# One kernel, two edits: decay attention's norm and sending steps in other slots, and the squares of the local and sink norms summed in four column groups of TensorE

## The chip, the cores and the metric

One core of one Trainium2 chip runs the whole program. The metric is device time of one execution in microseconds (us). The engines are named as in the profile: PE is TensorE's matrix multiplication and PEld its weight loads, DVE is VectorE, ACT is ScalarE, POOL is GpSimd, SP is SyncE, which here only issues DMAs.

## The reference

A chain of sixteen residual blocks on an array of 4096 tokens of 128 channels, `x = x + block(_layernorm(x))`. Three kinds of block matter here.

```
def _layernorm(x, axis=-1, eps=1e-05):
    m = jnp.mean(x, axis=axis, keepdims=True)
    v = jnp.var(x, axis=axis, keepdims=True)
    return (x - m) / jnp.sqrt(v + eps)

# local attention (L0_ffn): run twice, two layers each time
    x = x + local_attention(...) @ wo
    h = shift_token(x)
    h = (h - mu) / jnp.sqrt(var + 1e-05) * lg + lb      # norm of the half step
    ...

# decay attention (L1_attn_b), followed by a mixture of experts (L1_ffn)
    scores = jnp.einsum('bqhd,bkhd->bhqk', q, k) * scale
    decay = jnp.exp(-alpha * lag * DT)
    attn = jax.nn.softmax(scores * decay, axis=-1)

# sink attention (L2_attn_b)
    x = rmsnorm(h, attn_norm_scale)
    h = h + attention(x, ..., sinks)
    x = rmsnorm(h, moe_norm_scale)
```

## The kernel before

Tokens stand along the free axis: a tile is 128 channels (partitions) by 512 tokens, and there are eight such chunks, `NCH = 8`. The stages run one after the other as in the reference. Inside a stage the order of the work is written out by hand: a loop over slots, in each of which a few steps of different chunks are recorded, and every engine executes its own instructions in the recorded order. So a step's place in that order decides what is queued behind it on each engine.

A norm is three steps. `centre_step` (line 1759) multiplies a chunk by `cent` (identity minus 1/128) on PE, copies the result out of PSUM on ACT and squares it, on POOL or, with `square=True`, on ACT. `spread_step` (line 1774) multiplies the squares by `mean`, a 128 x 128 matrix of 1/128, on PE. So every one of the 128 output rows is the same row of 512 variances; ACT takes Ln and then Exp of minus one half of it, on 128 x 512 each, into the tile `nrs`. The third step, `scale`, multiplies the chunk by `nrs` on DVE.

Local attention is `local_attend` (line 3358). One slot `m` is half a batch: scores, weights, an output, projections for later slots, and at its end `chunk_steps(m)`. There a chunk's norm steps stand in three successive slots: slots 9, 10, 11 plus 4c for the norm of x (`norm_x_step`, chunks 5 to 7 and only in the first layer of a pair, since the stage before has done chunks 0 to 4), and slots 6 to 9 plus 4c for the norm of the half step (`norm_of_half`, chunks 0 to 6; chunk 7's runs in `local_ffn`). The stage is run four times.

Sink attention is `window_attention` (line 3160). A slot `n` is one unit of 128 queries by 128 keys, 128 units in all, 16 to a chunk. `before(c, i)` are the three steps of the norm ahead of it, whose `spread_step` with `twice=True` makes two results (two Ln, two Exp); `after(c, i)` are those of the norm behind it.

Decay attention is `decay` (line 2952), with its slots in `small_stage` (line 2797). There are 64 units, 8 to a chunk, one scored per slot. Units of even slots (kind 0) are multiplied by the decay out of PSUM on DVE, four instructions of 128 x 512, and one slot later exponentiated on ACT in one of 128 x 2048; units of odd slots (kind 1) are exponentiated out of PSUM on ACT, four of 128 x 512. A chunk's steps stand in slots relative to its first unit: `guard` (two reductions on DVE) at 1, `project` at -6, and so on, and the norm of x at -9, -8, -7. When a chunk is finished, `out` adds it to x, and `lead`, here `Sending.steps` (line 3637), follows in eleven steps: norm (three), `compare`, `choose`, `place`, `turn`, and four of `scatter`, which send the chunk's tokens to the experts' rows by indirect DMAs on POOL. `compare` and `choose` rank the experts in a string of some twenty small DVE instructions. `later` (line 2816) places these steps at the slot of the chunk's last weighing plus 4, 5, ..., 14.

PSUM has eight banks, shared out per stage; in decay six serve scores and everything else, so PE can be little more than a slot ahead of the engines that empty them.

SP carries the weight loads of the stages (line 615), each waiting until the buffer of an earlier stage is free, and in the first local layer 66 copies that fill two rooms in HBM for the experts' rows (`fill_rooms`, line 2114).

Of the kernel before, what the change touches and what calls it, by code (L numbers as in the profile page):

```python
# [17 lines left out]
P = 128  # L18
B, T, C = 16, 256, 128
NT = B * T  # L20
CH = 512
NCH = NT // CH
# [1627 lines left out]
class Fast(Net):  # L1650
# [120 lines left out]
            self.gt(sq, dst, dst, ALU.mult)  # L1771
        return sq

    def spread_step(self, pool, sq, bank, eps="eps5", twice=False):


        pv = self.bank(bank)
        self.mm(pv, self.k["mean"], sq)
        out = []
        for n in range(2 if twice else 1):  # L1780
            rs = pool.tile([P, CH], F32, tag=f"nrs{n}", name="nrs", bufs=2)
            if n:
# [8 lines left out]
    def norm_steps(self, pool, src, dst, bank, g=None, b=None, eps="eps5", copy=None, square=False):  # L1791


        held = {}

        def centre():
            held[0] = self.centre_step(pool, src, dst, bank, copy, square)

        def spread():
            held[1] = self.spread_step(pool, held[0], bank, eps)  # L1800
# [10 lines left out]
    def norm_x_step(self, pool, c, i, bank="ps", copy=None):  # L1811

        if c in self.led:
            return
        if i == 0:
            s = self.chunk(c)
            self.norms[c] = self.norm_steps(pool, self.x[:, s], self.ha[:, s], bank, copy=copy)
        self.norms[c][i]()

    def slots(self, n, *steps, last=(), every=1):  # L1820
# [976 lines left out]
    def small_stage(self, w, units, steps, tiles, evict, finish=None, group=1):  # L2797

# [7 lines left out]
        nc = self.nc  # L2806
        many = 2 * len(units)
        with ExitStack() as st:
# [5 lines left out]
            steps = [(first + i * group, lambda c, i=i: self.norm_x_step(p, c, i, "s")) for i in range(3)] + list(steps)  # L2814

            def later(n, i, f, c):

# [87 lines left out]
            def out(args):  # L2905
                slot, c = args
                pz = self.bank("s")
                self.mm(pz, w["Wo"], ots.pop(c))
                x = self.x[:, self.chunk(c)]
                if "bo" in w:  # L2910
                    self.stt(x, pz, w["bo"], x, ALU.add, ALU.add)
                else:
                    self.tt(x, x, pz, ALU.add)
                for i, f in enumerate(lead):
                    later(slot, (2 if finish else 4) + i, f, c)

            order = [None, join, turn, out]
            with self.share(s=6, o=2), self.tc.manual_schedule():
# [33 lines left out]
    def decay(self, w):  # L2952
# [4 lines left out]
        with ExitStack() as st:  # L2957
# [58 lines left out]
                (-2, lambda c: queries_by_edge(c, 0)), (0, lambda c: queries(c, 1)), (2, lambda c: queries_by_edge(c, 1)),  # L3016
            ]
            units = [(0, 0, 0), (0, 1, 1), (1, 1, 0), (1, 0, 1)]
            self.small_stage(w, units, steps, tiles, evict)

    def guard(self, stage, c, q, k):
        self.peak(stage, 0, c, q)
# [137 lines left out]
    def window_attention(self, w, h, n1, ns2):  # L3160
# [3 lines left out]
        with ExitStack() as st:  # L3164
# [134 lines left out]
            def before(c, i):  # L3299

                s = self.chunk(c)
                if i == 0:
                    held["sq"] = self.centre_step(p1, self.x[:, s], h[:, s], "s", square=True)
                elif i == 1:
                    held["rs"] = self.spread_step(p1, held["sq"], "s", twice=True)
                else:
                    r1, r2 = held["rs"]
                    self.stt(n1[:, s], h[:, s], w["ns1"], r2, ALU.mult, ALU.mult)
                    self.tt(h[:, s], h[:, s], r1, ALU.mult)

            def after(c, i):

                s = self.chunk(c)
                if i == 0:
                    held["sq"] = p1.tile([P, CH], F32, tag="nsq", name="nsq", bufs=2)
                    self.act(held["sq"], h[:, s], AF.Square)
                elif i == 1:
                    held["rs"] = self.spread_step(p1, held["sq"], "s")
                else:
                    self.stt(n1[:, s], h[:, s], ns2, held["rs"], ALU.mult, ALU.mult)  # L3320

            with self.share(s=4, o=4), self.tc.manual_schedule():
                self.logs()
                for n in range(-14, len(units) + 16):
                    if 0 <= n < len(units):
                        score(n)
                        later(n + 1, masked, n)
                    for f, args in (*due.pop(n, []), *due.pop(("last", n), [])):
                        f(*args)
                    if n % 2:  # L3330
                        for i in (n - 3, n - 2):
                            if 0 <= i < len(units):
                                weigh(i, n)
                        continue
# [12 lines left out]

    def local_begin(self):
        pass
# [8 lines left out]
    def local_attend(self, w, z, hs, last):  # L3358
# [6 lines left out]
        with ExitStack() as st:  # L3365
# [156 lines left out]
            def chunk_steps(m):  # L3522

                def due(slot):
                    c, rest = divmod(m - slot, 4)
                    return c if rest == 0 and 0 <= c < NCH else None

                if not last:
                    for i in range(3):
                        if (c := due(i - 9)) is not None:  # L3530
                            self.norm_x_step(p, c, i, "w")
                for slot in (-6, 5):
                    if (c := due(slot)) is not None:
                        self.shift(hs[:, self.chunk(c)], z[:, self.chunk(c)])

                for i in range(4):
                    if (c := due(6 + i)) is not None and c < NCH - 1:
                        if i == 0:
                            steps[1] = self.norm_of_half(p, "w", w, hs[:, self.chunk(c)])
                        steps[1][i]()  # L3540

            with self.share(w=3, s=4, o=1), self.tc.manual_schedule():
# [21 lines left out]
                    if within(m + 5, NTILE):  # L3564
                        project(m + 5)

    def norm_of_half(self, pool, bank, w, s):

        held = {}

# [1 line left out]
            held[0] = self.centre_step(pool, s, s, bank)  # L3572

        def spread():
            held[1] = self.spread_step(pool, held[0], bank)

        return [
            centre, spread, lambda: self.stt(s, s, w["lg"], held[1], ALU.mult, ALU.mult),
# [265 lines left out]
```

## Time and profile before

| what | value |
|---|---|
| median of 3 runs | 4233.71 us (4231.14 to 4234.19) |
| the profiled execution | 4216.97 us |
| its span, first to last instruction | 4215.2 us |
| PE busy | 3849.9 us, 91% |
| DVE, ACT, POOL busy | 61%, 55%, 44% |
| TensorE clock granted, mean | 0.951 |

| stage, loop alone | from about, to about (us) |
|---|---|
| local attention, four times | 140 to 440, 520 to 790, 1140 to 1440, 1470 to 1750 |
| decay attention | 2173 to 2450 |
| sink attention | 2900 to 3345 |

How to read it: a group is all instructions of one line, engine and pair of operands; most instructions are recorded at the line of a small helper (L504 is `mm`, L528 `act`, L531 `tt`, L534 `gt` on POOL, L543 `stt`), so a group is known by its tiles. A float32 matmul shows as two PE records. In a timeline a line is one run of like instructions: start, duration of the run, engine, line, operands, how many records, and in brackets the idle time ahead of it with what ended it. In a table of stretches the columns are the stretch, its length, the busy time of PE, PEld, DVE, ACT and POOL with their numbers of instructions, the granted TensorE clock, the DMA engines' share and GB/s.

### The profile page before, as it was taken

To read this page: it belongs to the slowest core of one execution; us is meant where nothing else is said; L and a number is where in the kernel's file an instruction comes from. 1 tells how busy PE (TensorE), PEld (TensorE's weight loads), DVE (VectorE), ACT (ScalarE), POOL (GpSimd) and SP (SyncE) were. 2 spreads that over 40 slices of the span, in tenths; PEclk is the share of its full clock that TensorE was granted. 3 is DMA by queue.
4 is the path that set the end of the run, shared out by engine and by line. 5 is a ranking of instruction groups with operands and counts; after the bars stand their busy time and mean duration, and the time that the engine had idled before them with its cause. 6 is when DMAs were issued, how large, how long until landed. Compare 5 with 4: busy or idle time off the path is not lost. (4 is left out here: it accounts for less than half of the span.)

```text
span 4215.2 us, 73089 instructions
## 1 busy us (share of the span) xinstructions
PE 3849.9 (91%) x28742; PEld 2195.1 (52%) x28742; DVE 2557.5 (61%) x4503; ACT 2314.2 (55%) x4485; POOL 1854.9 (44%) x1632
## 2 busy tenths in 40 slices
PE   7999999988899999985989879888999999899878
PEld 3555466465465456554965469543444344455333
DVE  4775576364577377464346633556877677486474
ACT  6666466555766466553456634444555554774532
POOL 4764365232566176326433434454555454321251
PEclk8999999988999999997999979999999999999989
DMA  1800000000000000004920058100000000000000
GB/s 61 345 2 1 11 2 1 20 1 1 20 1 1 3 1 1 1 6 142 320 76 12 16 180 297 41 19 16 1 1 1 3 1 10 6 2 19 6 0 21
DMA packets 78400, 176.38 MB, mean 42 GB/s; under 512 B 12606, under 2 KB 39108, under 8 KB 77920
## 3 DMA queue, kind: packets, MB, share of 16 engines
q1 hardware_dynamic: 65568, 148.40, 10.2%
q0 software_dynamic: 9120, 18.51, 1.3%
q8 instruction: 229, 3.75, 0.4%
q10 hardware_dynamic: 3360, 4.72, 0.4%
q14 instruction: 123, 1.01, 0.1%
HBM read 118.28 MB, written 54.20 MB: 41 GB/s over the span
## 5 line engine op out<-in xcount | busy, mean ns | idle before, releaser
L528 ACT ACTIVATE pt<-ps 128x512 f32<-128x512 f32 x640 | 339.9, 600 | 327.6 <-PE ps L504 326.4
L504 PE MATMUL ps<-hb,w 128*128 128x512 f32 (+1 forms) x960 | 461.0, 613 | 3.7 <-issue 3.3
L504 PE MATMUL ps<-w,hb 128*128 128x512 f32 (+2 forms) x896 | 403.8, 572 | 23.5 <-DVE t L531 18.6
L534 POOL TENSOR_TENSOR t<-t,t 128x512 f32<-128x512 f32 x256 | 319.8, 1271 | 161.1 <-DVE t L531 140.6
L531 DVE TENSOR_TENSOR t<-ps,tab 128x512 f32<-128x512 f32 x512 | 317.7, 682 | 84.6 <-ACT sq L528 81.1
L534 POOL TENSOR_TENSOR t<-t,ss 128x1024 f32<-128x1024 f32 x128 | 243.7, 1904 | 192.8 <-ACT ss L528 191.6
L504 PEld LDWEIGHTS ps<-hb,w 128*128 128x128 f32 (+1 forms) x960 | 178.6, 190 | 259.6 <-issue 223.0
L528 ACT ACTIVATE qkt<-ps 128x512 f32<-128x512 f32 x256 | 140.5, 595 | 291.7 <-PE ps L508 291.7
L531 DVE TENSOR_TENSOR u<-u,ps 128x384 f32<-128x384 f32 (+1 forms) x206 | 121.8, 596 | 288.0 <-PE ps L508 186.4
L531 DVE TENSOR_TENSOR ot<-ps,rd 128x512 f32<-128x512 f32 (+2 forms) x224 | 143.3, 640 | 203.2 <-ACT rd L528 203.2
L534 POOL TENSOR_TENSOR nsq<-ha 128x512 f32<-128x512 f32 x112 | 123.5, 1103 | 320.6 <-ACT ha L528 308.6
L504 PEld LDWEIGHTS ps<-w,hb 128*128 128x128 f32 x896 | 157.1, 194 | 178.6 <-issue 125.5
L534 POOL TENSOR_TENSOR both<-pt 128x1024 f32<-128x1024 f32 x64 | 151.2, 2363 | 199.8 <-DVE pt L531 164.1
L504 PE MATMUL ps<-nsq,ct 128*128 128x512 f32 x368 | 203.1, 635 | 34.3 <-POOL nsq L534 30.4
L504 PE MATMUL ps<-ot,w 128*128 128x512 f32 x448 | 213.2, 610 | 17.7 <-DVE ot L531 9.8
L504 PE MATMUL ps<-xt,w 128*128 128x128 f32 x1704 | 221.3, 281 | 1.5 <-ACT xt L528 1.5
L2199 POOL DMA_INDIRECT back<-y,x x142 | 139.1, 980 | 184.1 <-DVE y L538 63.3
L504 PE MATMUL ps<-u,w 128*128 128x512 f32 (+1 forms) x448 | 215.4, 605 | 3.5 <-POOL u L534 3.5
L504 PEld LDWEIGHTS ps<-xt,w 128*128 128x128 f32 x1704 | 205.2, 195 | 2.9 <-ACT xt L528 2.9
L528 ACT ACTIVATE u<-ps,w 128x512 f32<-128x512 f32 x160 | 107.8, 685 | 179.6 <-PE ps L504 177.0
L528 ACT ACTIVATE nrs<-ps,ct 128x512 f32<-128x512 f32 x208 | 139.7, 683 | 103.4 <-PE ps L504 97.8
L3741 POOL DMA_INDIRECT rows<-out,idx x128 | 126.1, 985 | 155.0 <-ACT out L528 105.5
(362 smaller groups left out, 8880.2 us busy)
## 6 DMA issues: line engine op xcount, KB each, us to landing
w<-in_moe_x SPq DMA_DIRECT2D x142, 533.0 KB
rows<-t SPq DMA_DIRECT2D x64, 520.0 KB
x<-rows SPq DMA_DIRECT2D x142, 65.0 KB
w<-in_local_f SPq DMA_DIRECT2D x8, 659.5 KB
y<-back ACTq DMA_DIRECT2D x16, 256.0 KB
y<-back SPq DMA_DIRECT2D x16, 256.0 KB
w<-in_local_f SPq DMA_DIRECT2D x4, 658.5 KB
back<-y,x POOLq DMA_INDIRECT x142
```

What stands on the lines that cost most here:

```text
L504: self.nc.tensor.matmul(out, lhsT, rhs, start=start, stop=stop)
L528: self.nc.scalar.activation(out, in_, func, **kw)
L531: self.nc.vector.tensor_tensor(out, a, b, op)
L534: self.nc.gpsimd.tensor_tensor(out, a, b, op)
L2199: nc.gpsimd.indirect_dma_start(views[i], bass.IndirectOffsetOnAxis(ap=x[:, C : C + 1].bitcast(I32), axis=0), y, None, bounds_check=2 * NT ...
L3741: nc.gpsimd.indirect_dma_start(views[(c * 2 + k) * 4 + t], bass.IndirectOffsetOnAxis(ap=idx[:, k, t : t + 1], axis=0), out[:, k, t], None,)
```

## The change

`spread_step` gets a second form, `compact_spread`. It makes only 32 equal rows for each quarter of the 512 tokens: four matmuls of a 128 x 32 piece of `mean` with 128 tokens each, into four groups of 32 partitions of one bank, so that the variances of all 512 tokens stand in a 128 x 128 tile. Ln and Exp run on 128 x 128 into a new tile `nrow` (with `twice`, two Ln of 128 x 128 and one Exp of 128 x 256). Four DMAs from SP, each with every one of 32 rows read four times, then spread `nrow` over 128 partitions into `nrs`; with `twice` eight DMAs. `scale` is as before. The form is used in local attention for both norms (34 norms: 3 + 7 + 7 in each pair of layers) and in sink attention for `before` of chunks 1 to 7 and `after` of chunks 0 to 6 (14 norms). The steps of sink attention move: in `before` the centre and spread steps of chunks 1 to 7 stand two slots earlier, `scale` where it was, so four slots lie between spread and scale where two did; in `after` `scale` stands two slots later, but for the last chunk.

In decay attention the norm of x stands at -10, -8, -7 where it was at -9, -8, -7, and the eleven steps of `lead` at 4, 6, 7, 9, 11, 13, 14, 15, 16, 17, 18 where they were at 4 to 14, but for the last chunk, which keeps 4 to 14. No work is added or removed there.

```diff
-    def spread_step(self, pool, sq, bank, eps="eps5", twice=False):
+    def spread_step(self, pool, sq, bank, eps="eps5", twice=False, compact=False):
+        if compact:
+            return self.compact_spread(pool, sq, bank, eps, twice)
         pv = self.bank(bank)
         self.mm(pv, self.k["mean"], sq)
...
+    def compact_spread(self, pool, sq, bank, eps, twice):
+        nc = self.nc
+        pv = self.bank(bank)
+        for r in range(4):
+            nc.tensor.matmul(
+                pv[32 * r : 32 * r + 32, :P], self.k["mean"][:, :32], sq[:, r * P : r * P + P],
+                start=True, stop=True, skip_group_check=True,
+            )
+        many = 2 if twice else 1
+        rows = pool.tile([P, many, P], F32, tag="nrow", name="nrow", bufs=2)
+        self.act(rows[:, 0], pv[:, :P], AF.Ln, bias=self.k[eps])
+        if twice:
+            self.act(rows[:, 1], pv[:, :P], AF.Ln, scale=1.0 + 1e-5, bias=self.k["eps10"])
+        flat = rows.rearrange("p n t -> p (n t)")
+        self.act(flat, flat, AF.Exp, scale=-0.5)
+        out = []
+        for n in range(many):
+            rs = pool.tile([P, CH], F32, tag=f"nrs{n}", name="nrs", bufs=2)
+            for r in range(4):
+                nc.sync.dma_start(rs[:, r * P : r * P + P], rows[32 * r : 32 * r + 32, n][:, None].broadcast_to([32, 4, P]))
+            out.append(rs)
+        return out if twice else out[0]
...
+            norm_at = norm_at or [first + i * group for i in range(3)]
+            first = min(norm_at)
+            steps = [(norm_at[i], lambda c, i=i: self.norm_x_step(p, c, i, "s")) for i in range(3)] + list(steps)
...
-                    later(slot, (2 if finish else 4) + i, f, c)
+                    later(slot, lead_at[i] if lead_at and c < NCH - 1 else (2 if finish else 4) + i, f, c)
...
-            self.small_stage(w, units, steps, tiles, evict)
+            self.small_stage(
+                w, units, steps, tiles, evict, norm_at=(-10, -8, -7), lead_at=(4, 6, 7, 9, 11, 13, 14, 15, 16, 17, 18),
+            )
...
-                    held["rs"] = self.spread_step(p1, held["sq"], "s", twice=True)
+                    held["rs"] = self.spread_step(p1, held["sq"], "s", twice=True, compact=c > 0)
...
-                    held["rs"] = self.spread_step(p1, held["sq"], "s")
+                    held["rs"] = self.spread_step(p1, held["sq"], "s", compact=c < NCH - 1)
...
-                    c, u = divmod(n + 14, 16)
-                    if u in (0, 2, 4) and c < NCH:
-                        before(c, u // 2)
+                    c, u = divmod(n + 16, 16)
+                    if c == 0 and u in (2, 4, 6):
+                        before(c, u // 2 - 1)
+                    if u in (0, 2, 6) and 0 < c < NCH:
+                        before(c, (u + 1) // 3)
                     c, u = divmod(n - 24, 16)
-                    if u in (0, 2, 4) and 0 <= c < NCH:
-                        after(c, u // 2)
+                    if u in (0, 2, 6 if c < NCH - 1 else 4) and 0 <= c < NCH:
+                        after(c, (u + 1) // 3 + (u == 4))
...
-                            self.norm_x_step(p, c, i, "w")
+                            self.norm_x_step(p, c, i, "w", compact=True)
...
-                            steps[1] = self.norm_of_half(p, "w", w, hs[:, self.chunk(c)])
+                            steps[1] = self.norm_of_half(p, "w", w, hs[:, self.chunk(c)], compact=True)
```

More of the change, by code (lines that the diff above doesn't have):

```diff
@@ L1789, in spread_step, with norm_steps @@
         return out if twice else out[0]
-    def norm_steps(self, pool, src, dst, bank, g=None, b=None, eps="eps5", copy=None, square=False):
+    def compact_spread(self, pool, sq, bank, eps, twice):
[20 more added lines that the diff above has]
+        return out if twice else out[0]
+    def norm_steps(self, pool, src, dst, bank, g=None, b=None, eps="eps5", copy=None, square=False, compact=False):
         held = {}
@@ L1799, in spread @@
         def spread():
-            held[1] = self.spread_step(pool, held[0], bank, eps)
+            held[1] = self.spread_step(pool, held[0], bank, eps, compact=compact)
         def scale():
@@ L1809, in norm_steps, with norm_x_step @@
         return [centre, spread, scale]
-    def norm_x_step(self, pool, c, i, bank="ps", copy=None):
+    def norm_x_step(self, pool, c, i, bank="ps", copy=None, compact=False):
         if c in self.led:
@@ L1816, in norm_x_step @@
             s = self.chunk(c)
-            self.norms[c] = self.norm_steps(pool, self.x[:, s], self.ha[:, s], bank, copy=copy)
+            self.norms[c] = self.norm_steps(pool, self.x[:, s], self.ha[:, s], bank, copy=copy, compact=compact)
         self.norms[c][i]()
@@ L2795, in values_by_head, with small_stage @@
         )
-    def small_stage(self, w, units, steps, tiles, evict, finish=None, group=1):
+    def small_stage(self, w, units, steps, tiles, evict, finish=None, group=1, norm_at=None, lead_at=None):
         nc = self.nc
@@ L2813, in small_stage @@
             first = min(at for at, _ in steps) - 3 * group
-            steps = [(first + i * group, lambda c, i=i: self.norm_x_step(p, c, i, "s")) for i in range(3)] + list(steps)
+            norm_at = norm_at or [first + i * group for i in range(3)]
+            first = min(norm_at)
+            steps = [(norm_at[i], lambda c, i=i: self.norm_x_step(p, c, i, "s")) for i in range(3)] + list(steps)
             def later(n, i, f, c):
@@ L3565, in local_attend, with norm_of_half @@
                         project(m + 5)
-    def norm_of_half(self, pool, bank, w, s):
+    def norm_of_half(self, pool, bank, w, s, compact=False):
         held = {}
@@ L3574, in spread @@
         def spread():
-            held[1] = self.spread_step(pool, held[0], bank)
+            held[1] = self.spread_step(pool, held[0], bank, compact=compact)
         return [
```

## The prediction

> **What bounds the kernel now.** I read the shares of each engine first, then the three changed stages as stretches, then single timelines.
>
> ```profile
> PE 3849.9 (91%) x28742; PEld 2195.1 (52%) x28742; DVE 2557.5 (61%) x4503; ACT 2314.2 (55%) x4485; POOL 1854.9 (44%) x1632
> ...
> 140.00:440.00 300.00, 292.45 (x2698) 174.95 (x2697) 202.22 (x299) 189.08 (x421) 156.73 (x140) 1.00 0.24 92
> 2900.00:3300.00 400.00, 398.93 (x3040) 163.09 (x3040) 321.73 (x513) 207.37 (x453) 219.47 (x126) 0.99 0.00 1
> 2173.00:2201.00 28.00, 27.32 (x326) 14.17 (x318) 17.19 (x34) 21.72 (x34) 7.48 (x4) 0.87 0.01 2
> 2265.00:2303.00 38.00, 34.08 (x392) 18.75 (x384) 25.19 (x61) 25.37 (x40) 15.35 (x12) 0.96 0.05 15
> ```
>
> PE is busy 97% of a local stage and over 99% of sink attention, at full clock, with no other engine above 81%. There a microsecond off PE is a microsecond off the end. Decay differs: a chunk without sending steps (third row) takes 28 us, one with them (fourth) 38, of which PE idles 4 and runs below full clock. There a stall can be taken out.
>
> **The change, part by part. First the sum of squares.** PE in one local slot, then copies and their landing:
>
> ```profile
> 302.20 0.40 PE L3485 MATMUL ps<-pu,v 128*32 128x128 f32 x8
> 302.42 0.51 PE L3485 MATMUL ps<-pt,v 128*32 128x192 f32 x8
> ...
> 303.29 0.40 PE L3485 MATMUL ps<-pu,ct 128*32 128x128 f32 x8
> 303.62 1.09 PE L508 MATMUL ps<-ct,t 128*128 128x128 f32 x8
> ...
> 306.27 1.02 PE L504 MATMUL ps<-nsq,ct 128*128 128x512 f32 x2
> 307.13 1.02 PE L504 MATMUL ps<-w,hb 128*128 128x512 f32 x2
> ...
> 200.87 0.63 ACT L528 ACTIVATE nrs<-nrs 128x512 f32<-128x512 f32 x1
> 208.44 2.31 DVE L543 SCALAR_TENSOR_TENSOR hb<-hb,w,nrs 128x512 f32<-128x512 f32 x1
> ...
> 2479.75 0.35 SPq L2165 DMA_DIRECT2D x<-rows  x1
> ...
> 2481.76 0.45 PE L508 MATMUL ps<-ct,x 128*128 128x128 f32 x1 [11.55 <-DMA x<-rows]
> ```
>
> The product that goes is the `nsq,ct` line: 307.13 - 306.27 = 0.86 us of PE from start to next start. What comes is already in this stage: `pu,v` is four products of 32 columns with 128 tokens (eight records), 302.42 - 302.20 = 0.22 us. Going from 32-column products to a full one costs more: 303.62 - 303.29 = 0.33, so 0.11 for leaving the mode. Entering it has no clean row; between 0 and another 0.11, and where a neighbour is a 32-column product already, neither is paid. So a norm saves 0.86 - 0.22 - 0.22 = 0.42 at least, 0.64 at most; I take 0.53, the measured switch alone, because entering is not seen as a gap.
>
> Against this the Trainium skill, page TensorEngine Tiling (Array Packing), section Key Properties, says that a change of tiling mode drains TensorE. With the fixed part of a warm matmul from page TensorE: Matmul & The Clock Gate, section Single matmul latency, 398 cycles or 0.17 us, as an estimate of one drain, two switches would take 0.33 us, a norm would save 0.31, and 48 norms 15 us where my 0.53 gives 25. The trace's 0.11 decides for me.
>
> Local: 34 x 0.53 = 18 us. Of a stage 2.5% is PE idle already, and the first norm's four copies find SP still issuing the room fills (until 204.4 us, the DMA engines full until about 207.5), so `scale` at 208.44 may be up to 3 us late, once: I take 16, bounds 34 x 0.42 - 3 = 11 and 34 x 0.64 = 22. Sink: 14 x 0.53 = 7, bounds 6 and 9.
>
> ACT loses Ln 0.683 and Exp 0.629 (rows `nrs`) and gets Ln of 128 x 128 at 0.376 (row `rd<-ps,es`) and an Exp of at most 0.416 (row `rd<-rd` of 128 x 256); with `twice` 2.62 becomes 0.376 x 2 + 0.416 = 1.17. ACT stands at 52 to 63% in these stages, so I cost this at nothing; PE's work hides it.
>
> The new copies: each is 64 KB, issued in 0.33 to 0.35 us. No row has SBUF to SBUF; the nearest, `x<-rows` of 65 KB from HBM, is issued at 2479.75 and read by PE at 2481.76, 2.0 us. Four issues and a landing are 4 x 0.34 + 2.0 = 3.4 us. In the local stage Exp ends at 200.87 + 0.63 = 201.5 and `scale` starts at 208.44: 6.9 us of cover. In sink attention a slot is (3343 - 2911) / 128 = 3.4 us, and four slots now lie between, 13 us. Behind a late `scale` on DVE would stand the next slot's multiplications out of PSUM, and PE waits for those. Behind SP's waits stand only later weight loads; these wait for a stage's end anyway (performer's weights leave at 474.3, mix's at 3349.4, after the last norms), so SP's queue costs nothing. DVE and ACT get up to four DMA semaphores to wait for per norm, events of 0.04 to 0.05 us (rows of POOL's and PE's queues): 0.2 us on engines with room, nothing.
>
> **Decay.** The bad place of a full chunk:
>
> ```profile
> 2335.86 2.59 DVE L531 TENSOR_TENSOR ahead<-lg 128x256 f32<-128x256 f32 x1
> ...
> 2340.46 1.96 PE L504 MATMUL ps<-ha,w 128*128 128x512 f32 x4 [1.10 <-DVE ha L531]
> 2342.35 2.73 PE L504 MATMUL ps<-qx,kx 32*128 32x512 f32 x8
> 2345.48 0.19 PE L504 MATMUL ps<-both,before 128*128 128x32 bf16 x1 [0.40 <-DVE both L538]
> ...
> 2347.55 0.94 PE L508 MATMUL ps<-ct,raw 128*128 128x128 f32 x4 [1.71 <-ACT pt L528]
> ...
> 2348.00:2351.00 3.00, 3.00 (x38) 2.19 (x37) 0.73 (x4) 0.00 (x0) 0.00 (x0) 0.50 0.00 0
> ```
>
> DVE is busy without a break from 2335.6 to 2348.3. Modulo 8, with durations from this timeline, its load before is: slot 0, decay multiplications 2.5, masks 0.7, lead scale 0.7; slot 1, compare 3.6, turn 0.5, scale of x 0.7, guard 1.35; slot 2, multiplications 2.5, choose 2.9, raw copy 0.7; slot 3, place 1.2. Slots 1 and 2 hold 12.2 us of DVE, and PE with about 7 us of products (2338.28 to 2351.76 at full clock) is held 13.5. That costs 6.5 us, some 2 of them because the granted clock falls to 0.50 from about 2348 to 2351.7.
>
> After, compare stands in slot 3, choose in 5, place in 7, the lead's norm in 6, 0 and 1. Slots 0 to 2 hold 3.2 + 3.3 + 3.2 = 9.7 us of DVE; slots 3 to 5 hold compare 1.4 to 3.6, values 0.7, turn 0.5, then 3.2, then choose 2.9, turn 0.5, x 0.75: 9.9 to 12; slots 6 and 7 about 5. PE needs about 30 for the eight slots (the 28 of the third row, cold at its start, and 3.7 of sending products), 11 in slots 0 to 2 and 10 in 3 to 5, so DVE fits but for a remainder of up to 2 us. `ahead` took 2.59 beside POOL's `qx` and 0.42 in the stage's tail; moved off it, it should be short. ACT is worse: slot 0 now holds the x norm's Ln and Exp 1.3, the lead's 1.3, two copies of turn 1.1, masks 0.9, two more 1.0, and slot 1 its own 4.0: 9.6 us against 7.5 of PE, a stall of up to 2. POOL issues the same scatters, 1.0 us each, two slots' worth ahead of `qx`, which the next odd unit needs four or more slots later: covered.
>
> The chunks with sending take 34.2, 37.6, 37.7, 37.7, 34.2 and about 34 between guards; against 30.5 that is some 33 us lost. With 1.5 to 2 us left per chunk, 33 - 10 = 23 are won. The tail gives back: chunk 6's compare and choose come two and three slots later, and its eight scatters at 1.28 us apiece now end after chunk 7's could start (ACT's copies at 2467.5), 2.5 us late, as the experts' first loads wait for the last scatter. I take 20; bounds 31 and, if the ACT burst takes all and the tail 4, minus 4.
>
> On the clock the same page TensorE: Matmul & The Clock Gate, section What's actually happening, gives a half clock after an idle window of about 3.4 us. By that rule this place, whose longest idle is 1.71 us, should not fall at all; the row shows 0.50. By the rule the gain would be 2 us per chunk smaller; I go by the row.
>
> **Sum.** 16 + 7 + 20 = 43. The profiled execution of 4216.97 (span 4215.2, 1.8 around it) becomes 4174. The median, 4233.71, lies 16.7 above it, as I expect again: 4191. Bounds of the three: 11 + 6 - 4 = 13 and 22 + 9 + 31 = 62, so 4172 to 4221.
>
> **Rivals.** (A) Decay's stall moves to ACT: the burst of slots 0 and 1 takes the place of DVE's. For it: 9.6 us against 7.5. Against: ACT idled 6.0 us at 2353.5 and has slots 2 to 7 light. Gain 16 + 7 + 0 = 23: 4211. (B) PE isn't the true end in local: DVE at 67% and POOL set the slot, and freed PE time turns into idle. For it: waits of PE on ACT and DVE exist. Against: they are 7 us in 300. Gain 3 + 7 + 20: 4204. (C), the slower side: the four copies don't overlap but follow each other, 4 x (0.34 + 2.0) = 9.4 us against 6.9 of cover; each local norm holds DVE, and PE behind it, 2.5 us: 34 x 2.5 = 85, net +42, 4276. It decides from a landing of 6.9 + 43 / 34 = 8.2 us. For it: the copies share 16 engines. Against: the copies to HBM before 204 us run eight deep at 400 GB/s, so the queue overlaps them.
>
> **How the numbers follow.** Forecast 0.66, A 0.17, B 0.08, C or the like 0.09. About 0.2% (8.5 us) is what a measurement of this kernel can tell from no change. Forecast: faster. A: 0.13 faster, 0.04 same. B: 0.05 and 0.03. C: slower. Faster 0.84, same 0.07, slower 0.09. The range 4172 to 4221 leaves out C and the edges.
>
> **What would show it.** A mean line of eight records of 0.22 us in local and sink; local stages 4 us shorter each, sink 7; `scale` not released by a DMA, but for the first; guard to guard in decay 31 to 33 us and no 0.50 stretch within a chunk. It is wrong if DVE waits on `nrs` copies, if ACT's `pt` releases PE in decay's slots 1 and 2, or if the local stages keep their length with PE idle.

## The result and the profile after

| | before | after |
|---|---|---|
| median, shown with the result | 4235.76 us (20 runs) | 4222.44 us (20 runs) |
| ratio | | 0.9967, 95% interval 0.9961 to 0.9974 |
| profiled execution | 4216.97 us | 4218.15 us |

The change makes the kernel 13 to 14 us faster; 43 us were forecast, and 4222 lies just outside the range. The two profiled executions, shown side by side, show no gain at all. Why that is so turned out to be the main finding, so here it is first: **the profile of before and the profile of after come from two kinds of sets, in which the same program runs differently.** A set is a series of runs that were made together, before among them, on one chip. In some sets the median of the kernel before is 4234 to 4237 us (as in the table), in others 4213 to 4216, with the same instructions. The forecast was made from a profile of the second kind, and the times it was set against are of the first. The expectations below speak of chips. The record doesn't bear that out: it gives two sets that were made a quarter of an hour apart, one of each kind, the same chip number (13). If that number names one chip, the kind is no fixed property of a chip.

What tells the kinds apart in the profiles are waits whose end the trace puts down to `remote`, a releaser that it doesn't know: all profiles of the one kind have some of over 1 us, those of the other none. The kinds differ in the two places where POOL sends tokens by scatters. From local attention's last softmax sums to the experts' first product behind the linear layer it is 228 to 230 us without these waits and 238 to 243 with them. From decay's first guard to the experts' first product it is 307 to 309 and 318 to 321 us with decay's slots of before, 278 and 303 to 308 with those of after.

The page of after, its line of busy times and the new queue entry (engine, busy us, share of the span, instructions; then the kind of transfer, its number and size):

```profile
PE 3831.5 (91%) x29030; PEld 2182.7 (52%) x29030; DVE 2551.0 (61%) x4503; ACT 2281.8 (54%) x4478; POOL 1853.7 (44%) x1632
...
nrs<-nrow SPq DMA_DIRECT2D x220, 64.0 KB
```

TensorE is 18.4 us less busy than before (3849.9) and ACT 32.4 (2314.2), with 55 x 4 new copies. So the change does what it says. The stretches shown before, from the profile of after (us, then the busy time of PE, its weight loads, DVE, ACT and POOL with instructions, the granted clock, the DMA share, GB/s):

```profile
140.00:440.00 300.00, 286.95 (x2752) 172.10 (x2751) 199.89 (x298) 183.01 (x421) 156.81 (x140) 0.99 0.28 101
2900.00:3300.00 400.00, 398.80 (x3121) 163.73 (x3120) 323.92 (x517) 196.89 (x446) 220.23 (x127) 0.99 0.06 14
2173.00:2201.00 28.00, 27.33 (x326) 14.20 (x322) 17.03 (x34) 21.89 (x34) 7.65 (x4) 0.87 0.00 1
2265.00:2303.00 38.00, 34.38 (x382) 18.84 (x381) 24.62 (x60) 24.99 (x40) 14.54 (x13) 0.91 0.05 16
```

In the first local layer TensorE now idles 13 us where it idled 7.6; most of what is added is one stop at the first norm, shown below. Sink attention is as full as before. Decay's stretch still has a clock below 1 and some 3.6 us of idle time.

**Local, slot by slot.** Outside of decay and the expert dispatches the trace repeats to 0.01 us from run to run, so I could set the slots of one layer side by side, from the first softmax-sum product of a slot (`pt,ct`) to that of the next. Of the 34 compact norms 20 shorten their slot by 0.44 to 0.46 us, 4 (the one but last of each layer) by 0.21, 4 (the last of each layer) by nothing, and 6 by nothing. A slot of each main kind, timeline of PE (start, duration of the run, line, product, records, idle time before and what ended it), first in before:

```profile
231.08 1.02 PE L504 MATMUL ps<-x,ct 128*128 128x512 f32 x2
231.94 1.02 PE L504 MATMUL ps<-nsq,ct 128*128 128x512 f32 x2
232.80 1.02 PE L504 MATMUL ps<-w,hb 128*128 128x512 f32 x2
234.23 1.12 PE L504 MATMUL ps<-w,hb 128*128 128x512 f32 x2 [0.41 <-ACT ha L528]
...
239.50 1.02 PE L504 MATMUL ps<-w,hb 128*128 128x512 f32 x2
240.36 1.02 PE L504 MATMUL ps<-nsq,ct 128*128 128x512 f32 x2
241.22 1.88 PE L504 MATMUL ps<-w,hb 128*128 128x512 f32 x4
```

Then in after:

```profile
235.74 1.02 PE L504 MATMUL ps<-x,ct 128*128 128x512 f32 x2
236.69 0.42 PE L1798 MATMUL ps<-nsq,ct 128*32 128x128 f32 x8
237.05 1.12 PE L504 MATMUL ps<-w,hb 128*128 128x512 f32 x2
238.88 1.12 PE L504 MATMUL ps<-w,hb 128*128 128x512 f32 x2 [0.71 <-ACT ha L528]
...
244.15 1.02 PE L504 MATMUL ps<-w,hb 128*128 128x512 f32 x2
245.10 0.42 PE L1798 MATMUL ps<-nsq,ct 128*32 128x128 f32 x8
245.46 1.98 PE L504 MATMUL ps<-w,hb 128*128 128x512 f32 x4
```

In the lower slot the compact product holds TensorE 0.36 us (245.10 to 245.46) instead of 0.86, but the product ahead of it takes 0.95 instead of 0.86 (244.15 to 245.10), and the group behind it 1.98 instead of 1.88: 0.30 is saved. Another 0.15 comes from short waits further on in the slot that are gone with it. The upper slot has the centring product of x as well. There the next projection waits for a bank that ACT's copy `ha` frees; before, it waited 0.41 us for it (at 234.23), now 0.71 and a little more inside the group, and the slot keeps its 9.27 us. In a layer's last slot it is DVE's `ot` that TensorE waits for: 0.62 us before, 1.46 after.

**The first norm.** Its four copies, on SP's queue (issue time, duration of the four), and DVE behind them:

```profile
203.89 0.33 SPq L2154 DMA_DIRECT2D rows<-t  x1
205.35 4.71 SPq L1813 DMA_DIRECT2D nrs<-nrow  x4
```

```profile
207.38 0.69 DVE L531 TENSOR_TENSOR ot<-ps,rd 128x512 f32<-128x512 f32 x1 [0.83 <-ACT rd L528]
214.88 0.75 DVE L543 SCALAR_TENSOR_TENSOR hb<-hb,w,nrs 128x512 f32<-128x512 f32 x1 [6.82 <-DMA nrs<-nrow]
```

The copies leave behind the last room fill, one every 1.3 to 1.5 us, about as the fills ahead of them do, and the last one's issue ends at 210.06; `scale` starts 4.8 us later, at 214.88 instead of 208.44. The slot grows by 5.1 us here and by up to 5.7 in the other profiles. The four local layers change by +2.6 to +3.2, -2.5, -2.5 and -2.5 us: some -4.5 together, not -16.

### The profile page after: what moved, and what is told of

The parts are those of the page before. It is cut to its first block, busy times and chain, and to the rows that moved or that the text cites. A ratio compares the mean times of both kernels' runs of the same rounds, so it can differ in the third digit from the quotient of the medians.

```text
span 4216.4 us, 74153 instructions
## 1 busy us (share of the span) xinstructions
PE 3831.5 (91%) x29030; PEld 2182.7 (52%) x29030; DVE 2551.0 (61%) x4503; ACT 2281.8 (54%) x4478; POOL 1853.7 (44%) x1632
## 5 line engine op out<-in xcount | busy, mean ns | idle before, releaser
L3479 PE MATMUL ps<-qkt 64*128 64x192 f32 (+1 forms) x2048 | 181.8, 311 | 9.6 <-ACT rd L528 9.6
L504 PE MATMUL ps<-ha,w 128*128 128x512 f32 x320 | 176.1, 672 | 11.6 <-ACT f L528 10.2
L504 PE MATMUL ps<-nsq,ct 128*128 128x512 f32 x272 | 154.5, 652 | 30.8 <-POOL nsq L534 26.6
```

The lines of the kernel that those rows point to most:

```text
L504: self.nc.tensor.matmul(out, lhsT, rhs, start=start, stop=stop)
L3479: nc.tensor.matmul(out, kt[rows, g, t * P : t * P + P], qt[rows, g, t * P : t * P + wide], start=(i, t) == (0, 0), stop=i == 1, skip_group ...
```

## The experiments

Each kernel is the changed one with the edits named, unless before is named. Ratios are against before, in the same set of runs, with 95% intervals.

**e1 to e4: the parts, each alone, beside the whole.** e2 keeps only local's compact squares, e3 only decay's slots, e4 only the sink edits; e2 undoes, among others,

```diff
             self.small_stage(
-                w, units, steps, tiles, evict, norm_at=(-10, -8, -7), lead_at=(4, 6, 7, 9, 11, 13, 14, 15, 16, 17, 18),
-            )
+                w, units, steps, tiles, evict)
...
-                    held["rs"] = self.spread_step(p1, held["sq"], "s", compact=c < NCH - 1)
+                    held["rs"] = self.spread_step(p1, held["sq"], "s")
```

> The changed kernel as it is, once more, for a second profile of it. Theory (the parts gain what the first profile shows, local 12 us up to the experts behind linear, decay 4, sink 1, and some of it is given back where the scatters on POOL set the end): 10 to 18 us below before, about -14; POOL's scatters behind linear wait again for ACT's out, some 12 us in all, because the 15.4 us wait of DVE at the tile at is a part of the changed order. Rival (that wait, put down to remote, is chance, as the five remote waits stand in one profile only): the wait is gone in this profile, the first x<-rows load behind linear comes near 1960 us instead of 1970.1, and the profiled execution is some 10 us shorter than 4218.15.

> Compact squares in the two local layers alone; decay and sink as before. Theory: the local stages win 2.6 lost at the first norm, then about 3 to 7 each, 12 us in sum, and nearly all of the -14 of the whole change is theirs: -8 to -14. Rival (the scatters on POOL behind linear set the end whatever comes before, so the local gain is lost there): within 3 us of before. The forecast's term was -16.

> The other slots for decay's norm and sending steps alone; local and sink as before. Theory (the loop of chunks wins about 8 us and the later last chunk gives half of it back): -4, between -1 and -7, guard to guard 34 to 37 us in the chunks with sending. Rival A (the stall moves wholly to ACT's burst of slots 0 and 1, and the experts' end gives back the rest): within 2 us of before. The forecast's term was -20.

> Compact squares and the moved steps in sink attention alone; local and decay as before. Theory (the product after a compact one pays about 0.55 us more than it did, so that of 0.6 us per norm next to nothing is left): -1, between -2 and +1; sink from its first product to mix's weights 436 us, 1 shorter than before. Rival (the forecast: 14 norms win 0.53 us each): -7, and the stage 430 us.

Measured: e1 0.9965 (0.9953 to 0.9977); local alone 0.9998 (0.9989 to 1.0007); decay alone 0.9973 (0.9962 to 0.9983), -11 us; sink alone 1.0005 (0.9996 to 1.0014). So in this set decay brings nearly all of it, and my theory, that local brings it and decay 1 to 7 us, fell: I had compared the marks of after with those of the first profile of before, and these belong to two kinds of sets. The 4.5 us that the traces show for local lie at the edge of its interval. All four profiles have the waits named remote; the first profile of before has none.

**e5, e8, e9: are the remote waits chance, or the place of the instructions?** e5 is before once more (one run with its profile). e8 and e9 put 40 small products early, into before and into e3:

```diff
+                if c == 2:
+                    pz = self.bank()
+                    for _ in range(40):
+                        nc.tensor.matmul(pz[:, :1], self.ident, self.ident[:, :1], start=True, stop=True)
                 self.copy_out(c, self.x[:, self.chunk(c)], pt)
```

> The kernel before, unchanged, for a second profile of it. Theory (the first profile of before is a lucky execution, without the stalls of 6 to 17 us that every other profile has while POOL issues scatters): span 4230 to 4236, the first x<-rows load behind linear near 1980 us instead of 1970.5, and mix's weights behind decay near 2478 instead of 2462.1. Rival (before has no such stalls, the new profiles are of other programs): span within 4 us of 4215.2 and both marks within 3 us of the first profile.

> Before, with 40 products of one column added on TensorE behind the third chunk's transposes at about 14 us, where TensorE idled 5.2 us; their result isn't read. All the rest as before, but TensorE's stream of instructions is 160 records of products and weight loads longer ahead of everything. Theory (the stalls beside the scatters are TensorE waiting for its instructions, which are fetched in blocks by a DMA queue of their own, so what decides is where a block ends against the scatters): the stalls of TensorE behind linear and in decay's last chunks stand at other products, and the time moves by 4 to 15 us either way, most likely down. Rival (the stalls belong to the work around the scatters, not to where a block ends): they stay at the same products, and the time is 0 to 4 us above before.

> The other slots of decay alone, as in e3_decay, with the same 40 products added at about 14 us. Theory (a large part of decay's -11 is luck of where the blocks of instructions end): it loses 4 us or more of its gain against e8_pad, or gains as much more; the two differ by something else than 11 by at least 4. Rival (the slots themselves win 11): 9 to 13 us below e8_pad.

Before again: span 4228.7, with such waits. e8: 1.0005 (0.9996 to 1.0014). e9: 0.9975 (0.9966 to 0.9983), 11.3 us below e8. Moving TensorE's instructions by 160 records changes neither the time nor decay's gain; the theory that the place of blocks of instructions sets it fell.

**e6, e7: decay's two tables apart.** e6 passes `lead_at` alone, e7 `norm_at` alone.

> Decay's sending steps alone in their new slots (lead_at), the norm of x as before. Theory (what holds a chunk is DVE's load of compare and choose in slots 1 and 2, which these move): most of decay's gain, -7 to -11, the chunks with sending 34 to 36 us from guard to guard instead of 36 to 38. Rival (the norm of x, whose ha came 1.1 us late before ha's products, is what wins): -1 to -4, and chunks of 36 to 37.

> Decay's norm of x alone in its new slots (norm_at), the sending steps as before; the counterpart of e6_lead. Theory (the two parts add up to e3_decay): 4 to 7 us below before. Rival (the norm's part wins only once the sending steps are out of its way): within 2 us of before.

e6: 0.9987 (0.9978 to 0.9997), some 5.5 us, between the two theories. e7: 1.0003 (0.9994 to 1.0012), nothing, and that in a set of the other kind; its chunks take 34.3 to 37.4 us like before's. So the norm's new slots win nothing alone, and the sending steps alone win half of what both win together in a set with remote waits (e3, 11 us). What the sending steps win alone without these waits was not measured.

**e10: local mended, with decay's slots and sink as before.** The first norm keeps its full product, and x is centred ahead of the softmax sums with the copy on DVE:

```diff
-                    for i in range(3):
+                    for i in (1, 2):
                         if (c := due(i - 9)) is not None:
                             self.norm_x_step(p, c, i, "w", compact=True)
...
-                            steps[1] = self.norm_of_half(p, "w", w, hs[:, self.chunk(c)], compact=True)
+                            steps[1] = self.norm_of_half(p, "w", w, hs[:, self.chunk(c)], compact=c > 0 or self.warm)
+                            self.warm = True
...
+                    if not last:
+                        c, rest = divmod(m + 9, 4)
+                        if rest == 0 and 0 <= c < NCH:
+                            self.norm_x_step(p, c, 0, "w", copy=self.nc.vector.tensor_copy, compact=True)
                     if within(m - 1, NTILE):
                         inverse(m - 1)
                         divide(m - 1)
```

> Decay's slots as changed, sink attention as before, and local compact with two mends: the very first norm keeps its full product (its copies waited behind the room fills), and the centring of x in a local layer's slots is issued ahead of the softmax sums, its copy out of PSUM on DVE instead of ACT. Theory (the slots in which x is centred win nothing because TensorE waits there for a PSUM bank that ACT's late copy ha frees; the first norm costs 5.7 us): the first local layer ends 8 us earlier than in e1_after, slots of 9.27 us become 8.2 to 8.9, and the whole is 5 to 9 us below e3_decay, about 4217. Rival (what holds these slots is ACT's whole load, not the place of ha): they stay at 9.2 to 9.3, the gain is the 5.7 of the first norm alone, and the whole is some 4220.

0.9892 (0.9877 to 0.9907): 46 us below before, which took 4212.54 here. The slots of 9.27 us fall to 8.29, and the four layers shorten by 4.9, 2.4, 5.4 and 2.3 us, 15 together; the stop of the first norm is gone, and so is every wait on `ha`. So both causes named above are shown by their removal; e10 moves the centring and its copy at once, so which of the two frees the slot is not. But 15 and 11 are not 46. The rest is decay: its chunks with sending take 30.5 to 32.4 us here, where all profiles of e3 and e9 had 33 to 37, and this profile has no remote wait. e7 and e11, of the same set, have none either.

**e12 to e16: chip or kernel?** All on unchanged texts: after (e12), decay alone (e13), e10 again (e14), before (e15, one run with its profile), in one set; then after alone (e16).

> The changed kernel a third time, beside e13 to e15 on one chip. Theory (the waits named remote come with the chip or what else runs on it, not with a kernel): either all four profiles of this call have them or none; with them 10 to 18 us below before, without them 25 to 38 below, decay's chunks 30 to 33 us. Rival (they come with the layout of the kernel): this profile has them as after and e1_after had, and the time is some 14 below before, while e14_mend has none.

> Decay's slots alone, again. Theory (chip): with remote waits -11 as in e3_decay, without them -20 to -30. Rival (layout): -11 in both cases.

> e10_local_mend again. Theory (chip): if this call has remote waits, decay's chunks are 33 to 37 us and the kernel is 14 to 19 us faster than e13_decay by its local layers alone, some -25 to -30 against before; if it has none, -44 to -48 as in e10. Rival (layout): -44 to -48 in any case, decay's chunks 30.5 to 32.4.

> The kernel before, for a profile beside the others. Theory (chip): remote waits if the other three have them, and then decay's chunks of 36.3 to 38.5 us; none if they have none, and then 34.2 to 37.7. Rival (layout): as the first profile of before, none, in any case.

> The changed kernel once more, for a chip without the waits named remote. Theory: before runs at 4205 to 4218 there, decay's chunks with sending take 30.5 to 32.4 us, and the change wins 28 to 36 us (decay some 30, local 4, sink 0 to 1). If before runs at 4228 to 4240 again, it is a chip with these waits, and the change wins 10 to 18. Rival (decay's gain in e10 came from its local mends): 10 to 18 in any case.

The set of e12 to e15 has remote waits, in all four profiles: after 0.997 (0.9958 to 0.9981), decay 0.9974 (0.9963 to 0.9984), and e14, the same text as e10, 0.9941 (0.9929 to 0.9954), 25.5 us instead of 46. e16's set is without them (before 4215.83 there): after takes 4182.53, **0.9922 (0.9908 to 0.9936), 33 us faster.** So the waits come with the set and not with the kernel: the rival of layout is out. The set of e10, without them, and that of e12 to e15, with them, are the two with the same chip number, so whether it is the chip, what else ran beside it or something that changed in between stays open.

The same place of a decay chunk of the same program in both kinds of sets. First after, ACT and then POOL:

```profile
2327.57 0.37 ACT L528 ACTIVATE ot<-ps 128x256 f32<-128x256 f32 x1
2330.51 0.60 ACT L528 ACTIVATE raw<-ps 128x512 f32<-128x512 f32 x1 [2.57 <-PE ps L504]
2331.00 0.68 ACT L528 ACTIVATE nrs<-ps,ct 128x512 f32<-128x512 f32 x1
2331.72 0.63 ACT L528 ACTIVATE nrs<-nrs 128x512 f32<-128x512 f32 x1
2332.25 0.89 ACT L528 ACTIVATE qz<-q,ct 128x256 f32<-128x256 f32 x2
```

```profile
2326.22 1.01 POOL L3773 DMA_INDIRECT rows<-out,idx  x1 [1.69 <-ACT out L528]
...
2330.10 0.97 POOL L3773 DMA_INDIRECT rows<-out,idx  x1 [0.30 <-issue]
```

Then e16:

```profile
2316.24 0.37 ACT L528 ACTIVATE ot<-ps 128x256 f32<-128x256 f32 x1
2316.50 0.59 ACT L528 ACTIVATE raw<-ps 128x512 f32<-128x512 f32 x1
2317.27 0.69 ACT L528 ACTIVATE nrs<-ps,ct 128x512 f32<-128x512 f32 x1 [0.17 <-PE ps L504]
2317.99 0.63 ACT L528 ACTIVATE nrs<-nrs 128x512 f32<-128x512 f32 x1
2318.53 0.89 ACT L528 ACTIVATE qz<-q,ct 128x256 f32<-128x256 f32 x2
```

```profile
2314.88 1.01 POOL L3773 DMA_INDIRECT rows<-out,idx  x1 [1.69 <-ACT out L528]
```

What `raw` reads was complete at 2327.5 in after (its last `pt,vo` product ended then), yet ACT starts it at 2330.51, 4.29 us after POOL's first scatter of four; in the same three chunks of e1 that distance is 4.23 to 4.26 and in those of e9 4.34 to 4.36. In e16 it starts at once, 1.62 us after the first scatter in every chunk. Behind it stand the two `nrs`, `qz` and four exponentials on ACT, and TensorE waits for `raw`, `qz` and the exponentials, as PE of after and then of e16 shows:

```profile
2328.49 1.14 PE L504 MATMUL ps<-qx,kx 32*128 32x512 f32 x8
2331.16 0.66 PE L508 MATMUL ps<-ct,raw 128*128 128x128 f32 x4 [1.53 <-issue]
2331.74 1.08 PE L2894 MATMUL ps<-pt,vo 128*32 128x128 f32 x32
2332.76 3.02 PE L504 MATMUL ps<-qz,k 32*128 32x512 f32 x8
```

```profile
2317.16 1.14 PE L504 MATMUL ps<-qx,kx 32*128 32x512 f32 x8
2318.23 0.66 PE L508 MATMUL ps<-ct,raw 128*128 128x128 f32 x4
2318.82 1.08 PE L2894 MATMUL ps<-pt,vo 128*32 128x128 f32 x32
2319.83 2.21 PE L504 MATMUL ps<-qz,k 32*128 32x512 f32 x8
```

A group's duration hides a wait inside it: eight records of `qz,k` need 1.14 us when nothing holds them (as those of `qx,kx`), so 3.02 is 1.9 of waiting, for the exponentials that empty the banks one after the other. That is 1.5 + 0.8 us more per chunk than in e16, at this place alone.

**e11, e17, e18: why sink attention wins nothing.** e11 has only the sink edits, and issues the squares' product ahead of the slot's projections. e17 is e10 with compact squares in sink attention too, but the steps in their old places; e18 is e10 again, in the same set as e17. The edit of e11 (its helper `held_norms` calls `before` and `after` with the changed places, the spread steps only where its second argument is true, the others where it is false):

```diff
+                    held_norms(n, True)
                     i, step = divmod(n + 8, 8)
                     if 0 <= i < 2 * NCH:
                         prepare(i, step // 2, n)
...
+                    held_norms(n, False)
```

> Sink attention alone, compact as in e4_sink, but the product of the squares is issued ahead of the slot's projections instead of behind them, so that the scores behind it no longer take the PSUM bank that DVE empties last. Theory (the slot with a mean is set by DVE emptying four projection banks, and the compact product only made TensorE wait 0.55 us in the scores): the slots with a mean fall from 7.10 and 7.24 us to 6.6 to 6.8, the stage is 5 to 7 us shorter than in e4_sink, the whole 4229 to 4232. Rival (changing from 32-column products to the 64-row products of the scores costs the 0.55): the wait goes with the product to its new neighbours, and the slots stay at 7.1 to 7.2.

> e10_local_mend with compact squares in sink attention too, but its norms' steps in their old places (scale one pair of slots behind the squares, not two). Theory (the moved steps brought the mean in front of scores that take its bank): the scores behind a compact product take 1.13 us again, the slots with a mean 6.7 us, the stage is 6 to 7 us shorter than in e18_mend. Rival (the compact product itself ends so early that whatever scores follow wait for ACT's logarithm behind it): 1.5 to 1.7 us again, and the stage within 1.5 us of e18_mend; if the copies are late for the earlier scale, longer than that.

> e10_local_mend a third time, as the ground for e17_sink_old on the same chip: -25 to -27 us against before where the remote waits stand, -44 to -48 where they don't.

e11: 1.0003 (0.9994 to 1.0012); half its slots with a mean fall to 6.93 us, half stay at 7.2. The product after the compact one, now a full projection, takes its usual 1.98 us: a change of tile mode doesn't cost the 0.55. e17: 0.9924 (0.9911 to 0.9938), 4203.91 beside e18's 4210.30 (0.9938, 0.9925 to 0.9952), 6.4 us faster. Sink attention itself, from its first projection to mix's weights, takes 463.56 us instead of 467.73 in the two profiles: 4.2 of it, and the rest is within the intervals. One norm ahead of attention in before, PE:

```profile
2969.12 1.02 PE L504 MATMUL ps<-nsq,ct 128*128 128x512 f32 x2
2970.07 1.13 PE L504 MATMUL ps<-q,k 64*128 64x512 f32 x4
```

The two kinds of norm in e17, ahead of attention and behind it, PE and then ACT:

```profile
2955.51 0.42 PE L1798 MATMUL ps<-nsq,ct 128*32 128x128 f32 x8
2955.86 1.13 PE L504 MATMUL ps<-q,k 64*128 64x512 f32 x4
...
2976.56 0.43 PE L1798 MATMUL ps<-nsq,ct 128*32 128x128 f32 x8
2976.92 1.68 PE L504 MATMUL ps<-q,k 64*128 64x512 f32 x4
```

```profile
2956.57 0.61 ACT L528 ACTIVATE nrow<-ps,ct 128x128 f32<-128x128 f32 x2
...
2977.05 0.37 ACT L528 ACTIVATE nrow<-ps,ct 128x128 f32<-128x128 f32 x1 [0.20 <-PE ps L1798]
```

The lower scores (1.68) are 0.55 us longer than the upper, and 2976.92 + 0.55 = 2977.47 is 0.05 us after ACT's logarithm ends (2977.05 + 0.37). In e11 they took 1.37, and 3040.95 + 0.24 = 3041.19 is 0.04 after the logarithm ended there too. So the second of the two score products, which otherwise run side by side, waits until ACT has read the mean. Its records say the same: in six of the seven such norms of e17, and in twelve of the fourteen norms of e11, it starts 0.04 us after the ACT semaphore that it waits for was raised by that logarithm. In the upper pair it doesn't: it runs while ACT reads. In their old places the norms ahead of attention win 0.50 each (two slots of together 6.33 us become 5.83), those behind it nothing (7.19, 7.24). With the moved steps both kinds wait, but not for the same thing. A moved norm ahead of attention in after, PE and then DVE:

```profile
2963.00 0.42 PE L1798 MATMUL ps<-nsq,ct 128*32 128x128 f32 x8
2963.36 1.54 PE L504 MATMUL ps<-q,k 64*128 64x512 f32 x4
```

```profile
2962.92 0.74 DVE L543 SCALAR_TENSOR_TENSOR q<-ps,w 128x512 f32<-128x512 f32 x1
```

Here the second score product starts at 2963.81, and what it waits for, by its records, is a semaphore that DVE raises at 2963.67, when it has emptied a projection's bank. That is what e11's theory had supposed for all of them; it holds for this kind alone. Why the scores depend on that logarithm in the one place and not in the other (which bank each gets) was not tried.

## Why the prediction was right or wrong

**The base: wrong, and it decides.** "The median, 4233.71, lies 16.7 above it, as I expect again". The 16.7 us weren't an offset around the profile but other stage times: remote waits of 1 to 17 us beside POOL's scatters. A profile outside the span of its own kernel's times (4216.97 against 4231.14 to 4234.19) is of something else, and that was to be seen beforehand. Where before takes about what its profile took, 4216 us, the change wins 33 us, inside the bounds of 13 to 62; where the median was taken, it wins 13 to 14, at their lower end. That 33 is nearer to the 43 than the parts are is luck: decay won 10 more than forecast, local and sink 18 less.

**Decay: right in mechanism, but 30 or 11 us where 20 were forecast.** The bounds were 31 and -4. In e16 the stage gains 33 us from its first guard to mix's weights against the first profile of before, and the last scatters take 2.9 of it back (2.5 forecast); chunks are 30.6 to 32.4 us (31 to 33 forecast), and no stretch at a clock of 0.50 is left within one. DVE's stall goes and what is left is ACT's burst: `qz,k` waits 1.07 us. In the sets with remote waits it is 11 (e3, e9, e13), in part because ACT starts `raw` 2.5 us late in the burst of slots 0 and 1. That is rival A's place: I had its queue right, but not what would come into it.

**Local: 16 forecast, some 4.5 measured.** The price of one product was too good: 0.30 are saved by the product and its two switches, below my bound of 0.42, since the eight records' 0.22 grow by some 0.33 in all; with the small waits a free slot wins 0.45. The Trainium skill, page TensorEngine Tiling (Array Packing), section Key Properties, says that changing the tiling mode drains TensorE; the estimate made from it with page TensorE: Matmul & The Clock Gate, section Single matmul latency, was a saving of 0.31, and the trace now agrees with it rather than with the 0.11 for a switch that I took from a row. The step that failed is "34 x 0.53", which took each slot's end to be TensorE's. In ten slots it isn't, and four more win half: what ended them was ACT's `ha` (six), DVE's `ot` (four, the last of each layer) and, in the last but one, ACT's `rd`. The waits on ACT's `ha` stood in the profile of before, as 1.2 us in three slots of the first layer; I had weighed them by their sum (rival B, "7 us in 300") instead of asking which slots they end. The second miss is "up to 3 us late, once": `scale` came 6.4 us late and the slot grew by 5.1 to 5.7, since four copies behind the fills took 4.71 us to issue instead of 1.4 and landed 4.8 us after the last issue's end. The price of an issue was too low in any case: 0.54 to 0.67 us each, not 0.33 to 0.35. Elsewhere four mostly leave in 2.5 us, and where DVE waits for the copies (four times in after, 0.9 us on average) `scale` starts 4.2 to 5.0 us after Exp's end, not 3.4. That is far below the 8.2 at which rival C would have decided, and its 85 us did not come.

**Sink: 7 forecast, 0 to 1 measured.** The step that failed is "14 x 0.53". That PE is busy "over 99% of sink attention" was read as TensorE being the end. Busy time includes waits inside a group, so a saved 0.5 us can come back in the next group as longer scores, and did: 1.54 and 1.68 us instead of 1.13.

## What to carry to other kernels

Before adding terms, look whether the profiled execution lies among the kernel's own times; if not, the stages have other lengths there than where the gain is measured. A saving on the busiest engine counts slot by slot: in each slot with an edit look which wait ends it, however small their sum is over the stage. Put new transfers away from a burst on the same queue. Behind a product whose result another engine must read, look at what the next products into the same pool of banks wait for.

The version that came out best keeps the first norm full, centres x earlier on DVE, has decay's new slots and the sink steps in their old places: e17, 4203.91 us, 33 below before in a set with remote waits, where the change as given wins 12 to 15. Without sink's compact squares (e10) it wins 46 in a set without these waits; e17 was not run in one.

## What the hardware showed unexpectedly

- The same program in two kinds of sets: the medians of after are 4220 to 4223 us in the one and 4182.53 in the other, those of before 4234 to 4237 and 4213 to 4216; the granted clock is nearly the same (mean 0.950 and 0.954 in the profiles of after and e16). In the first kind waits that the trace ends with remote, or with an engine long done, stand beside streams of scatters, the longest behind the linear layer, where ACT stood still for up to 16.9 us (e4) and DVE for 15.4. One of after, DVE:

```profile
1944.67 0.19 DVE L531 TENSOR_TENSOR at<-ps,place 128x32 f32<-128x32 f32 x1 [15.44 <-remote]
```

  What delays them was not found: not the place of the instructions (e8, e9), and no packet of the two instruction queues lies in the wait of e9 at 2336 us.
- Four copies of 64 KB within SBUF mostly leave in 2.5 us, but took 4.71 us directly behind the room fills: one every 1.3 to 1.5 us, about as the fills themselves (one every 1.3 to 1.9).
- Away from the scatters and the first copies, nearly all slots of local attention repeat to 0.01 us from run to run and from set to set, so 0.05 us per slot can be read from two single profiles.
